# Moving the one-hots ahead of the exps and the column copies in ScalarE's round of a graph attention kernel

## Chip, cores and metric

The kernel runs on one core of one Trainium2 chip. The metric is the device time of one launch in microseconds (us); the time of a kernel is the median of its runs. The kernel before took 1878.13 us (three runs, 1872.55 to 1889.53).

## What is computed

One layer of graph attention with a residual and a layer norm. There are 6250 nodes with 128 features (8 heads of 16) and 206250 edges, sorted by the node they lead to (`dst`). Cut to what matters:

```python
Qh, Kh, Vh = (h @ W for W in (WQ, WK, WV))          # 6250 x 8 x 16 each
Eh = edge_attr @ WE                                  # 206250 x 8 x 16
score = einsum('ehd,ehd,ehd->eh', Kh[src], Qh[dst], Eh) / sqrt(16)
score = exp(clip(score, -5, 5))
msg = Vh[src] * score[:, :, None]
wV, Z = segment_sum(msg, dst), segment_sum(score, dst)
out = layernorm(x + wV / (Z + 1e-6))
```

## The kernel before

**Tiles and rounds.** The edges are cut into 1612 tiles of 128, and these into 406 batches, nearly all of 4 tiles. A table of K and V rows for all nodes (`kv`) is made at the start. Then the loop at L755 makes one round per batch. A round does not finish its batch: the work on a batch is spread over several rounds, so that in round b the engines stand at different batches:

- TensorE (`stage_a`, L608) multiplies the transposed one-hots of batch b with rows of Q into `qps`, and the edge features with WE into `eps`. `stage_0` (L555) makes the marks of batch b-1, one matmul for two batches, so in every second round; `stage_0t` (L588) makes `marks_t` of batch b+2. Marks are numbers that are 1 where an edge leads to a node of the window and not above 0 elsewhere. `finish` (L664) folds the sums of finished windows into one block of 128 nodes (`finps`, mostly 12 or 14 matmul records in the rounds that have it). `stage_c` (L683) adds the messages of batch b-3 into `agg`. `project_columns` (L493) makes K and V of one tile of batch b+2 (`colkv`), and `q_rows` (L341) now and then a block of Q rows (`qrows`).
- VectorE makes `kq` of batch b-1 (L627, L629), sums and clips the scores of batch b-2 (L636, L639) and makes the messages of batch b-3 (`msg`, L678). In between it copies columns of x (L449), splits a block of Q rows (`qst`, L348 to L351) and does pieces of layer norms.
- ScalarE takes the exps of batch b-2 (`weigh`, L642: once into `exp_p`, once beside the messages), copies `colkv` to where batch b+1 expects it (`place_columns`, L503, the copy at L507), copies some 26 columns of x into `xcol` (`columns`, L454), and turns marks into one-hots by a Relu: `mark` (L572, `onehot` of batch b-1 and the next) and `mark_t` (L600, `onehotT` of batch b+2). Behind these come the copy of a fold (`fin`, L671), of a finished pair of windows (`sum`, L711) and of single rows (L491).
- GpSimd gathers rows of `kv` for the tiles of batch b+2 (L518), one indirect DMA per tile. A gather does not start before `qps` of a batch some rounds back is done (L522; the distance shrinks from 12 batches to 3 along the run). SyncE issues the loads.

**Columns.** For 5 of 11 batches the last tile is not gathered. Its 128 source nodes are columns of x that lie on the chip; ScalarE copies 58 of them one by one and VectorE 70 in pairs, and `colkv` is their product with the weights. Columns run ahead: those of a batch are due some four rounds before `project_columns` uses them. Every 16 columns the numbers are read into registers (L420).

**Order and buffers.** From batch 12 on the order of each engine is the order in which the loop's code is written (L758), and each engine works through it strictly. Semaphores set by the framework make an instruction wait for its inputs and for its output's buffer. Four small pools of PSUM matter here: `exp_p` exists once, so the exps of batch b-2 wait for the messages of batch b-3; `eps` once, so it waits for `kq` (L629) of the batch before; `marks_t` once, so it waits for the `onehotT` of the round before. `marks`, `finps`, `colkv` and `qrows` share two buffers in turn (tag `oT`): each waits until what was put there two before has been read, marks by `onehot`, finps by `fin`, colkv by the copy at L507, qrows by `qst` and `qr` on VectorE.

Of the kernel before, what the change touches and what calls it, by code (L numbers as in the profile page):

```python
# [146 lines left out]
def edge_attention(ctx: ExitStack, tc: tile.TileContext, x, xT, srcT, srcA, srcV, srcR, dstT, dstB, dst0, bnd, loB, onB, onQ, eaT,  # L147
# [29 lines left out]
    nbat = len(batches)  # L177
# [9 lines left out]
    with ExitStack() as fast:  # L187
# [167 lines left out]
        def build_q(until, now):  # L355

            while qwork or (now and len(built) < until):
                if not qwork:
                    qwork.append([q_rows(len(built)), 0])
                qwork[0][1] += 1  # L360
                if next(qwork[0][0], None) is None:
                    qwork.pop()
                if not now:
                    break
# [67 lines left out]
        def due(b, v, part):  # L432

            n = int((b + part - 1 - COL0 + COLL) * COLP[1] * share[v] / COLP[0] + 1e-6) // (1 + v) * (1 + v)
            return min(n, len(col_batches) * share[v])

        def copy(v):

            c, (k, i) = copied[v] % COLN, divmod(copied[v], share[v])
            if c == 0:  # L440
                addresses(v)
                at_hand[v] = ahead[v].pop(0)
            copied[v] += 1 + v
            if k not in col_tiles:
                col_tiles[k] = wp.tile([P, P], F32, name="xcol", bufs=6)
            to, at = col_tiles[k], at_hand[v]
            if v:
                i += share[0]
                nc.vector.tensor_tensor(to.bitcast(I32)[:, i:i + 2], column(at[c], 8, I32),  # L449
                                        column(at[c + 1], 8, I32), op=ALU.bitwise_or)  # L450
            else:
                nc.scalar.copy(to[:, i:i + 1], column(at[c], 4, F32))  # L452

        def columns(b, part=1.0):  # L454

            while copied[0] < due(b, 0, part):
                copy(0)
# [45 lines left out]
        def place_columns():  # L503

            while projected:
                g, pk = projected.pop()
                nc.scalar.copy(g[:, B - 1, :], pk)  # L507
# [64 lines left out]
        def mark(b):  # L572

            if b not in marks:
                return
            m, oh, h, n, k = marks.pop(b)
            base = oh[:, h, :n, HW * h:HW * h + HW]
            if k == 2:
                (p_, *dims) = [list(x) for x in base.ap]
                base = bass.AP(tensor=base.tensor, offset=base.offset, ap=[p_, [B * P + HW, 2], *dims])  # L580
                m = m.rearrange("p (k b) w -> p k b w", k=2)
            else:
                m = m[:, :n]
            nc.scalar.activation(base, m, AF.Relu)  # L584
# [3 lines left out]
        def stage_0t(b):  # L588

            if b in marks_t or b in ohTs:  # L590
                return
            t0, n = batches[b][0], len(batches[b])
            m = psM.tile([QROWS, B * P], F32, name="marks_t")
            for i in range(0, n * P, WT * P - t0 % WT * P):
                e0 = (t0 * P + i) % (WT * P)
                w = min(n * P - i, WT * P - e0)
                nc.tensor.matmul(m[:, i:i + w], steps_q, rels[(t0 * P + i) // (WT * P)][:, e0:e0 + w], start=True, stop=True)  # L597
            marks_t[b] = m, n

        def mark_t(b):  # L600

            if b not in marks_t:
                return
            m, n = marks_t.pop(b)
            ohTs[b] = wp.tile([QROWS, B * P], BF16, name="onehotT", bufs=4)
            nc.scalar.activation(ohTs[b][:, :n * P], m[:, :n * P], AF.Relu)  # L606
# [35 lines left out]
        def weigh(b):  # L642

            n, g, sc = st8[b]
            nc.scalar.activation(exp_p[:, :n], sc[:, :n], AF.Exp, scale=0.25)  # L645
            m = wp.tile([P, B, MW], F32, name="msg")
            nc.scalar.activation(m[:, :n, D:], sc[:, :n], AF.Exp, scale=0.25)  # L647
            st8[b] = [n, g, m]
# [15 lines left out]
        def finish(q):  # L664

            ps = psT.tile([P, MW], F32, name="finps", tag="oT")
            add_windows(ps, q, True, True)
            if q % 2 == 0:
                fins[q] = sp.tile([P, 2, MW], F32, name="fin", bufs=2)
            fin = fins[q - q % 2]  # L670
            nc.scalar.copy(fin[:, q % 2], ps)  # L671
            if q % 2:
                q -= 1
                pending.append(layernorm(nc, sp, fins.pop(q), xbs.pop(q), out, q, 2, stores))

        def messages(b):
            n, g, m = st8[b]
            nc.vector.tensor_tensor(  # L678
                m[:, :n, :D].rearrange("p b (h d) -> p b h d", h=H),
                g[:, :n, D:].rearrange("p b (h d) -> p b h d", h=H),  # L680
                exp_p[:, :n, :, None].to_broadcast([P, n, H, DH]), op=ALU.mult)
# [73 lines left out]
        for b in range(nbat + 4):  # L755
# [52 lines left out]
            next(summed, None)  # L808
            if 0 <= b - 3 < nbat:
                messages(b - 3)  # L810
            if 0 <= b - 2 < nbat:
                weigh(b - 2)
            while qwork and b > XB and qwork[0][1] < 3:
                build_q(0, False)
            place_columns()
            if 0 <= b - 1 < nbat:
                stage_0(b - 1)
            if b + 2 < nbat:
                stage_0t(b + 2)
            if b < nbat:  # L820
                columns(b)
            mark(b - 1)
            if b + 2 < nbat:
                mark_t(b + 2)
            for _ in range(len(ready) if b >= nbat - 2 else 1):
                if ready:
                    finish(ready.pop(0))
# [206 lines left out]
```

## Time and profile before

| | |
|---|---|
| median of three runs | 1878.13 us |
| the profiled execution | 1871.11 us, its span 1869.3 us |
| busy, share of the span: PE, VectorE, ScalarE, GpSimd | 80%, 88%, 80%, 73% |
| column copies on ScalarE (L452) | 9802 of 189 ns, 991.4 us |
| onehot (L584), onehotT (L606) on ScalarE | 206 of 577 ns, 406 of 581 ns |
| the exps (L645, L647) | 406 of 199 ns, 406 of 218 ns |
| copy of colkv (L507) | 169 of 358 ns |
| mean granted TensorE clock | 0.931 |

The kernel has three stages: the table (to about 160 us), the rounds with columns (to about 1800 us), and the drain. A row of the waits gives the waiting engine, operation and line, then what ended the wait, and then the total, the number and the longest wait in us. A row of the timeline gives start and length in us, engine, line, operation, what it writes and reads, how many instructions are merged, and in brackets the idle time before it with what ended that. On one engine, neighbours can overlap by about 0.1 us. A row of the windows gives the stretch, its length, busy us (and instructions) of PE, the weight loads PEld, VectorE (DVE), ScalarE (ACT) and GpSimd (POOL), and then the granted clock, the share of DMA time and GB/s.

### The profile page before, as it was taken

To read this page: it belongs to the slowest core of one execution; us is meant where nothing else is said; L and a number is where in the kernel's file an instruction comes from. 1 tells how busy PE (TensorE), PEld (TensorE's weight loads), DVE (VectorE), ACT (ScalarE), POOL (GpSimd) and SP (SyncE) were. 2 spreads that over 40 slices of the span, in tenths; PEclk is the share of its full clock that TensorE was granted. 3 is DMA by queue.
4 is the path that set the end of the run, shared out by engine and by line. 5 is a ranking of instruction groups with operands and counts; after the bars stand their busy time and mean duration, and the time that the engine had idled before them with its cause. 6 is when DMAs were issued, how large, how long until landed. Compare 5 with 4: busy or idle time off the path is not lost.

```text
span 1869.3 us, 54198 instructions
## 1 busy us (share of the span) xinstructions
PE 1499.8 (80%) x10000; PEld 1206.9 (65%) x10000; DVE 1648.0 (88%) x8774; ACT 1495.3 (80%) x11631; POOL 1359.8 (73%) x1433
## 2 busy tenths in 40 slices
PE   6898878878787888888887878877888878777886
PEld 4676657666666666666676666756766656666765
DVE  6468998898889988999989999899899899999986
ACT  3446888788898888898888888888888988988962
POOL 7767767777777776777766777777777777777774
PEclk9888898899899998999989999899989999999897
DMA  8655556556555655655555556556555556566652
GB/s 292 214 163 161 163 173 188 165 179 183 170 178 177 183 172 162 184 180 174 181 173 163 177 174 183 176 167 177 173 174 180 179 175 185 177 178 183 198 153 67
DMA packets 169255, 329.59 MB, mean 176 GB/s; under 512 B 67440, under 2 KB 95156, under 8 KB 168904
## 3 DMA queue, kind: packets, MB, share of 16 engines
q0 software_dynamic: 67664, 183.79, 33.0%
q1 hardware_dynamic: 100115, 141.48, 24.9%
q14 instruction: 272, 2.22, 0.4%
q8 instruction: 80, 1.31, 0.3%
q10 hardware_dynamic: 1124, 0.79, 0.1%
HBM read 309.03 MB, written 16.88 MB: 174 GB/s over the span
## 4 chain that ended last, share of the span: by engine, by line
DVE 34%; ACT 17%; PE 13%; DMA 8%; issue 7%; DVEq 6%; POOL 4%; SPq 2%; ACTq 2%; POOLq 0%
ACT xcol L452 12%; DVE xcol L449 10%; DMA kvrows<-kv,src 7%; DVEq L420 6%; DVE kq L629 5%; DVE sc L636 5%; DVE msg L678 5%; DVE kq L627 5%; POOL kvrows L518 4%; PE agg L700 4%; PE eps L620 3%; ACT onehot L584 2%; PE finps L659 2%; ACT onehotT L606 2%; ACTq L420 1%
## 5 line engine op out<-in xcount | busy, mean ns | idle before, releaser
L518 POOL DMA_INDIRECT kvrows<-kv,src x1378 | 1309.8, 950 | 471.6 <-issue 308.0
L452 ACT COPY xcol<-xz 128x1 f32 x9802 | 991.4, 189 | 76.9 <-issue 66.9
L700 PEld LDWEIGHTS agg<-msg,onehot 128*128 128x128 f32 x3224 | 436.0, 203 | 318.3 <-DVE msg L678 119.1
L449 DVE TENSOR_TENSOR xcol<-xz 128x2 int32 x5915 | 508.9, 152 | 60.5 <-issue 58.3
L620 PE MATMUL eps<-we_sb,ea 128*128 128x128 f32 x3224 | 489.4, 298 | 71.8 <-DVE kq L629 69.8
L700 PE MATMUL agg<-msg,onehot 128*128 128x136 f32 x3224 | 518.5, 307 | 32.3 <-DVE msg L678 30.6
L620 PEld LDWEIGHTS eps<-we_sb,ea 128*128 128x128 f32 x3224 | 424.2, 205 | 100.4 <-DVE kq L629 94.5
L627 DVE TENSOR_TENSOR kq<-kvrows,qps 128x512 f32<-128x512 f32 x406 | 273.8, 674 | 63.5 <-PE qps L615 38.8
L597 PE MATMUL marks_t<-rows_q,steps_q 5*126 5x512 bf16 x406 | 161.8, 399 | 169.5 <-ACT onehotT L606 155.5
L629 DVE TENSOR_TENSOR kq<-kq,eps 128x512 f32<-128x512 f32 x406 | 271.1, 668 | 8.6 <-PE eps L620 6.5
L678 DVE TENSOR_TENSOR msg<-kvrows,exp_p 128x512 f32<-128x512 f32 x406 | 272.7, 672 | 6.2 <-ACT exp_p L645 6.2
L636 DVE TENSOR_REDUCE sc<-kq 128x32 f32<-128x512 f32 x406 | 271.9, 670 | 0.3
L606 ACT ACTIVATE onehotT<-marks_t 126x512 bf16<-126x512 f32 x406 | 235.9, 581 | 19.2 <-PE marks_t L597 18.9
L645 ACT ACTIVATE exp_p<-sc 128x32 f32<-128x32 f32 x406 | 80.9, 199 | 193.9 <-DVE msg L678 191.1
L615 PE MATMUL qps<-qw,onehotT 126*128 126x128 bf16 x1612 | 168.8, 229 | 10.9 <-DVE kq L627 10.9
L615 PEld LDWEIGHTS <-onehotT 126*128 126x128 bf16 x1612 | 134.5, 103 | 47.8 <-issue 21.7
L500 PE MATMUL colkv<-wkv_sb,xcol 128*128 128x256 f32 x338 | 116.2, 429 | 17.2 <-ACT onehot L584 17.2
L584 ACT ACTIVATE onehot<-marks 128x512 f32<-128x512 f32 (+2 forms) x206 | 119.0, 577 | 5.5 <-PE marks L563 5.4
L659 PEld LDWEIGHTS finps<-sum,shift 128*128 128x128 f32 x640 | 81.4, 198 | 40.3 <-ACT kvrows L507 20.9
L659 PE MATMUL finps<-sum,shift 128*128 128x136 f32 x640 | 91.4, 296 | 9.5 <-ACT kvrows L507 9.5
L647 ACT ACTIVATE msg<-sc 128x32 f32<-128x32 f32 x406 | 88.5, 218 | 0.0
L639 DVE TENSOR_SCALAR sc<-sc 128x32 f32<-128x32 f32 x406 | 80.9, 199 | 0.9
(88 smaller groups left out, 799.3 us busy)
## 6 DMA issues: line engine op xcount, KB each, us to landing
ea<-eaT SPq DMA_DIRECT2D x201, 512.0 KB
rowkv<-kv SPq DMA_DIRECT2D x2176, 1.0 KB
kvrows<-kv,src POOLq DMA_INDIRECT x1378
qw<-qs SPq DMA_DIRECT2D x202, 31.5 KB
kv<-ea SPq DMA_DIRECT2D x12, 512.0 KB
qs<-qst SPq DMA_DIRECT2D x48, 96.0 KB
rows_q<-relD SPq DMA_DIRECT2D x202, 6.0 KB
rows<-relO SPq DMA_DIRECT2D x202, 6.0 KB
```

The source lines that it names most:

```text
L449: nc.vector.tensor_tensor(to.bitcast(I32)[:, i:i + 2], column(at[c], 8, I32), column(at[c + 1], 8, I32), op=ALU.bitwise_or)
L452: nc.scalar.copy(to[:, i:i + 1], column(at[c], 4, F32))
L518: ins = nc.gpsimd.indirect_dma_start(out=g[:k, i, :f], out_offset=None, in_=rows, in_offset=bass.IndirectOffsetOnAxis(ap=src_col(t)[:k], a ...
L606: nc.scalar.activation(ohTs[b][:, :n * P], m[:, :n * P], AF.Relu)
L615: expanded[b] = nc.tensor.matmul(pq[:, i, :], ohT[:, i * P:i * P + P], loaded[t0 // WT], start=True, stop=True)
L620: nc.tensor.matmul(pe[:, i, :], ea[:, i * P:i * P + P], we_sb, start=True, stop=True)
L627: nc.vector.tensor_tensor(t0[:, :n], g[:, :n, :D], pq[:, :n], op=ALU.mult)
L629: nc.vector.tensor_tensor(t0[:, :n], t0[:, :n], pe[:, :n], op=ALU.mult)
L636: nc.vector.tensor_reduce(sc[:, :n], t0[:, :n].rearrange("p b (h d) -> p b h d", h=H), axis=AX.X, op=ALU.add)
L659: nc.tensor.matmul(ps, shift[:, P - s:2 * P - s], sums[k // 2][:, k % 2], start=first and i == 0, stop=stop and i == len(parts) - 1)
L678: nc.vector.tensor_tensor(m[:, :n, :D].rearrange("p b (h d) -> p b h d", h=H), g[:, :n, D:].rearrange("p b (h d) -> p b h d", h=H), exp_p[ ...
L700: nc.tensor.matmul(aggs[u][:, 0 if final else k % 2], oh[:, i, :], m[:, i, :], start=not final and t % (2 * G) == 0, stop=tail)
```

## The change

Within a round the calls of `mark` and `mark_t` come ahead of `weigh`, `place_columns` and `columns`. The matmuls that make the marks (`stage_0`, `stage_0t`) keep their place in TensorE's order. `finish` and `stage_c` come behind all of them as before.

```diff
             if 0 <= b - 3 < nbat:
                 messages(b - 3)
-            if 0 <= b - 2 < nbat:
-                weigh(b - 2)
             while qwork and b > XB and qwork[0][1] < 3:
                 build_q(0, False)
-            place_columns()
             if 0 <= b - 1 < nbat:
                 stage_0(b - 1)
             if b + 2 < nbat:
                 stage_0t(b + 2)
-            if b < nbat:
-                columns(b)
             mark(b - 1)
             if b + 2 < nbat:
                 mark_t(b + 2)
+            if 0 <= b - 2 < nbat:
+                weigh(b - 2)
+            place_columns()
+            if b < nbat:
+                columns(b)
             for _ in range(len(ready) if b >= nbat - 2 else 1):
                 if ready:
                     finish(ready.pop(0))
```

The orders of TensorE, VectorE, GpSimd and SyncE are the same in both kernels; only ScalarE's differs. First, ScalarE in the middle of the run, in the round with the marks that are made at 1243 us in the trace and the start of the next round. Before:

```order
L711 COPY sum<-agg 128x272
L645 ACTIVATE exp_p<-sc 128x32
L647 ACTIVATE msg<-sc 128x4x8
L420 TENSOR_LOAD col_at_82
L452 COPY xcol<-xz 128x1 x16
L420 TENSOR_LOAD col_at_82
L452 COPY xcol<-xz 128x1 x11
L584 ACTIVATE onehot_79<-marks 128x2x4x64
L606 ACTIVATE onehotT<-marks_t 126x512
L671 COPY fin<-finps 128x136
L645 ACTIVATE exp_p<-sc 128x32
```

Now:

```order
L711 COPY sum<-agg 128x272
L584 ACTIVATE onehot_79<-marks 128x2x4x64
L606 ACTIVATE onehotT<-marks_t 126x512
L645 ACTIVATE exp_p<-sc 128x32
L647 ACTIVATE msg<-sc 128x4x8
L420 TENSOR_LOAD col_at_82
L452 COPY xcol<-xz 128x1 x16
L420 TENSOR_LOAD col_at_82
L452 COPY xcol<-xz 128x1 x11
L671 COPY fin<-finps 128x136
L606 ACTIVATE onehotT<-marks_t 126x512
```

The same 27 columns now stand behind both one-hots, the copy of the fold follows the columns directly, and the next round begins with its onehotT and not with its exp.

Second, ScalarE in the round whose marks are made at 801 us, where a colkv of the round before is copied. Before:

```order
L452 COPY xcol<-xz 128x1 x4
L606 ACTIVATE onehotT<-marks_t 126x512
L711 COPY sum<-agg 128x272
L645 ACTIVATE exp_p<-sc 128x32
L647 ACTIVATE msg<-sc 128x4x8
L507 COPY kvrows<-colkv 128x256
L452 COPY xcol<-xz 128x1 x12
```

Now:

```order
L452 COPY xcol<-xz 128x1 x4
L711 COPY sum<-agg 128x272
L584 ACTIVATE onehot_77<-marks 128x2x4x64
L606 ACTIVATE onehotT<-marks_t 126x512
L645 ACTIVATE exp_p<-sc 128x32
L647 ACTIVATE msg<-sc 128x4x8
L507 COPY kvrows<-colkv 128x256
L452 COPY xcol<-xz 128x1 x12
```

Between the columns of one round and the copy of colkv (L507) in the next stood one onehotT, of the round before; now onehot and onehotT of the round itself stand there.

## Prediction

> **What bounds the kernel now.** I read the page first, then the busy times of the long middle stage in one piece (160 to 1800 us: all but the table at the start and the drain), then the waits inside that stage, and last the timeline of single rounds.
>
> ```profile
> span 1869.3 us, 54198 instructions
> 160.00:1800.00 1640.00, 1325.01 (x9004) 1068.49 (x9005) 1502.95 (x8411) 1413.58 (x11398) 1205.76 (x1271) 0.94 0.59 176
> DVE xcol L449 <- issue: 56.6, 112, 1.3
> DVE qst L348 <- PE qrows L344: 36.7, 28, 2.5
> DVE kq L627 <- PE qps L615: 25.5, 25, 2.6
> ACT exp_p L645 <- DVE msg L678: 146.8, 123, 4.1
> PE marks_t L597 <- ACT onehotT L606: 154.3, 161, 2.3
> PE qrows L344 <- ACT onehot L584: 21.0, 17, 2.3
> PE colkv L500 <- ACT onehot L584: 17.2, 17, 2.2
> 1001.75 0.95 POOL L518 DMA_INDIRECT kvrows<-kv,src  x1 [0.30 <-issue]
> 1003.00 0.94 POOL L518 DMA_INDIRECT kvrows<-kv,src  x1 [0.30 <-issue]
> ```
>
> In the second row the columns after the length are PE, PEld, DVE, ACT and POOL busy. VectorE works 1503 of 1640 us and spends 57 more on reading column numbers into registers ("issue"). What is left of its idle time is almost only two waits: qst for qrows and kq for qps, 36.7 + 25.5 = 62.2 us. It hardly ever waits for ScalarE directly. GpSimd stands close behind: a gather starts every 1.25 us (1001.75 to 1003.00), and 1271 of them fill 1589 us, so the stage cannot become more than about 51 us shorter however well the rest runs. ScalarE waits 147 us for VectorE and has room. So the time is VectorE's work plus the 62 us in which it waits for TensorE, and the question is what the new order on ScalarE does to those 62 us. TensorE's 154 us of waiting for onehotT is the largest number here, but TensorE is busy 1325 of 1640 us and most of that wait is covered: only what reaches qst or kq counts.
>
> **The change part by part.** Nothing is added or removed; every instruction of TensorE, VectorE, GpSimd and SyncE keeps its place. On ScalarE the ring of work is almost the same ring; what differs is that the one-hots of this round now stand ahead of the exps, so they are a round's columns earlier, and exps, the copy of colkv (L507) and columns stand behind them. A fold (finps) and its copy (fin) keep their place behind the columns.
>
> I sorted rounds 31 to 379 by what TensorE issues in them and added up the two VectorE waits that follow each kind. Where the waits are large, TensorE has a long round, because finps, colkv or qrows come on top. The first kind, ten rounds with finps and colkv, 13.1 us in all, looks like this:
>
> ```profile
> 1243.11 0.38 PE L563 MATMUL marks<-steps,rows 26*128 26x512 bf16 x1
> 1243.13 0.68 DVE L678 TENSOR_TENSOR msg<-kvrows,exp_p 128x512 f32<-128x512 f32 x1
> 1243.64 1.66 PE L659 MATMUL finps<-sum,shift 128*128 128x136 f32 x12
> 1245.14 1.09 PE L700 MATMUL agg<-msg,onehot 128*128 128x136 f32 x8
> 1247.11 0.67 DVE L678 TENSOR_TENSOR msg<-kvrows,exp_p 128x512 f32<-128x512 f32 x1
> 1247.75 0.58 ACT L584 ACTIVATE onehot<-marks 128x512 f32<-128x512 f32 x1
> 1248.24 0.57 ACT L606 ACTIVATE onehotT<-marks_t 126x512 bf16<-126x512 f32 x1
> 1248.39 0.70 PE L500 MATMUL colkv<-wkv_sb,xcol 128*128 128x256 f32 x2 [2.16 <-ACT onehot L584]
> 1249.35 0.69 DVE L627 TENSOR_TENSOR kq<-kvrows,qps 128x512 f32<-128x512 f32 x1 [1.57 <-PE qps L615]
> ```
>
> The marks are ready at 1243.49, but their one-hot comes at 1247.75 behind 27 columns, and colkv needs its PSUM buffer. With the one-hot first it starts near 1243.5, colkv at 1246.2 behind agg, and kq at 1247.8 instead of 1249.35. Over the ten rounds I leave 4.6 us (two are late for other reasons): **-8.5 us**.
>
> ```profile
> 244.45 0.29 DVE L348 CAST qst<-qrows 128x128 bf16<-128x128 f32 x1 [0.93 <-PE qrows L344]
> 1706.86 0.29 DVE L348 CAST qst<-qrows 106x128 bf16<-106x128 f32 x1 [0.47 <-PE qrows L344]
> 365.17 0.29 DVE L348 CAST qst<-qrows 128x128 bf16<-128x128 f32 x1 [2.09 <-PE qrows L344]
> 1598.59 0.29 DVE L348 CAST qst<-qrows 128x128 bf16<-128x128 f32 x1 [2.00 <-PE qrows L344]
> 1018.26 0.51 PE L344 MATMUL qrows<-wq_sb,xz 128*128 128x128 f32 x2
> 1017.95 0.26 ACT L671 COPY fin<-finps 128x136 f32<-128x136 f32 x1
> ```
>
> The first two rows are the first and last of twelve rounds with colkv and qrows and no finps, 11.2 us: here qrows takes the buffer of the marks, the same cure holds: agg and colkv behind one msg and then qrows take some 2.4 us, and the next msg, behind which qst stands, ends 4 us later (1243.81 and 1247.78 above), so nothing is left: **-11 us**. The next two are the first and last of eight rounds that have finps, colkv and qrows, 15.8 us. There qrows takes the buffer of finps, and the last two rows show it start as soon as fin ends (1018.21). fin stays behind the columns. Counted from the end of the last columns, three one-hots stood ahead of it (onehotT, then the exps and columns, then onehot and onehotT) and now two do; each takes 0.49 (1247.75 to 1248.24). So fin comes 0.5 us earlier, eight times: **-4 us** of 15.8.
>
> A third sort of wait has nothing to do with long rounds:
>
> ```profile
> 316.00:318.00 2.00, 0.28 (x3) 0.22 (x2) 2.00 (x15) 1.81 (x15) 1.70 (x2) 1.00 0.72 234
> 320.00:322.00 2.00, 2.00 (x11) 1.64 (x10) 0.75 (x3) 1.96 (x16) 1.47 (x2) 0.50 0.44 126
> 318.44 0.37 PE L597 MATMUL marks_t<-rows_q,steps_q 5*126 5x512 bf16 x1 [2.16 <-ACT onehotT L606]
> 321.92 0.69 DVE L627 TENSOR_TENSOR kq<-kvrows,qps 128x512 f32<-128x512 f32 x1 [1.25 <-PE qps L615]
> ```
>
> TensorE waits 2.16 us for onehotT, its granted clock (third number from the end in the windows) then falls to 0.50, the products take nearly twice as long, and kq is late. Fourteen rounds of this sort hold 11.2 us. The wait at marks_t goes, since onehotT of the round before is now done before that round's columns. Bounds: nothing, if the slow clock alone makes kq late, and 11.2; I take half, **-5.5 us**, as in this row the wait is larger than what kq loses.
>
> Now the price. In 23 rounds finps takes the buffer of the last colkv and waits for ScalarE's copy L507 (upper rows: one of fifteen plain cases):
>
> ```profile
> 801.05 0.39 PE L563 MATMUL marks<-steps,rows 26*128 26x512 bf16 x1
> 801.78 0.20 ACT L645 ACTIVATE exp_p<-sc 128x32 f32<-128x32 f32 x1 [0.76 <-DVE msg L678]
> 801.92 0.21 ACT L647 ACTIVATE msg<-sc 128x32 f32<-128x32 f32 x1
> 802.04 0.35 ACT L507 COPY kvrows<-colkv 128x256 f32<-128x256 f32 x1
> 802.44 1.89 PE L659 MATMUL finps<-sum,shift 128*128 128x136 f32 x14 [0.79 <-ACT kvrows L507]
> 804.76 0.68 DVE L678 TENSOR_TENSOR msg<-kvrows,exp_p 128x512 f32<-128x512 f32 x1
> 805.58 0.69 DVE L627 TENSOR_TENSOR kq<-kvrows,qps 128x512 f32<-128x512 f32 x1
> ```
>
> ```profile
> 1748.94 0.37 ACT L507 COPY kvrows<-colkv 128x256 f32<-128x256 f32 x1
> 1750.02 0.38 PE L563 MATMUL marks<-steps,rows 26*128 26x512 bf16 x1
> ```
>
> Before, the exp starts when msg ends, at 801.78. Now onehot can start only at 801.44, when the marks are made, onehotT follows 0.49 later and the exp another 0.49 behind it, at 802.42: L507 ends 0.64 later than it did, and finps, agg, qps and kq shift with it, because kq already starts right behind msg here (805.44) with TensorE just in time. 23 x 0.64 = 14.7 us. In eight of the 23, TensorE was behind and L507 was over about when the marks began or before (the last of the eight is the lower pair); those lose up to 1.5 us, and I add 0.5 each: **+19 us**. The bounds are nothing (TensorE, freed of its waits, is early enough) and 23 x 1.5 = 35 us.
>
> The exps are later by the same 0.64 in rounds with marks. That is hidden: msg at 804.76 needs the second exp of 802.13, 2.6 us earlier. Without that cover it would cost 0.64 in every second round, over 100 us; I take **+2 us** for rounds in which ScalarE is already late. What else is queued behind the waiting onehot is the columns, ready some four rounds ahead of their use, and fin.
>
> The clock is the last term. The stage's mean granted clock is 0.94, so TensorE runs some 197 us at half speed (1640 x 0.06 x 2). Fewer waits should mean fewer such spells; between nothing and the 5.7 us left over above, I take **-4 us**. [...]
>
> Sum: -8.5 - 11 - 4 - 5.5 + 19 + 2 - 4 = -12 us. The profiled execution took 1871.1 us, 1.8 of it outside the span; so 1859 for such an execution. The median of the three runs shown is 1878.1, 7 us above it, and 12 off that median is **1866 us**, 0.6% less.
>
> **The rivals.** *The folds lose nothing* (0.22): TensorE, without the 154 us of waits and with the other 38 us for onehot gone, starts a fold's round early enough, and the +19 and +2 stay away; with half of the eight rounds behind fin cured as well (-4 more) and the clock better, 35 to 40 us go. For it: those waits are in four rounds of ten. Against it: the marks themselves come right behind eps, whose start VectorE sets, so in a round like that at 801 us TensorE cannot be earlier. 1840 us.
>
> *The clock decides* (0.12): if half of the 197 us at half speed disappear, the fourteen slow rounds lose all their 11.2 us and the long rounds gain another few; -12 becomes -20 to -24, 1856 us. [...] Against it: TensorE's work is the same, so its share of idle time hardly changes; waits for VectorE take the place.
>
> *ScalarE is now tied to TensorE* (0.16), the case on the other side: every exp, copy and column stands behind one-hots that wait for eps and marks. If the marks come 1 us or more behind msg (TensorE late, clock at 0.50) in the 23 folds, each loses the full 1.5 us (+35); in the ten rounds with finps and colkv and the eight behind fin the later fold eats the 12.5 us gained, and the slow rounds and the clock give nothing. Only -11 remain of the gains, and +24 us give 1902. With these gains gone it passes no change from 0.5 us per fold (11 / 23) and 1% from 1.3. For it: the order is exactly this. Against it: the row at 801 us, a plain one, gives 0.64.
>
> *It does nothing that shows*: the terms cancel. This lies inside my forecast, whose sum is small against its parts.
>
> **How the numbers follow.** My forecast has 0.50; its own range, with the fold term between 8 and 27 and the slow rounds between 0 and 11 us, is 1852 to 1880. The range takes in the first rival and half of the other side: 1839 to 1889. A measurement of this kernel can tell about 1% (19 us, below 1859 or above 1897). Faster by more: the first rival's 0.22, two thirds of the clock's 0.12 and 0.08 from the lower edge of the forecast, 0.38. Slower by more: the third rival without its lower edge, 0.14. Same: 0.48.
>
> **What would show it.** Right: PE marks_t waits for onehotT almost vanish (154 to under 20 us); colkv and qrows hardly wait for onehot; qst for qrows falls from 36.7 to about 20; finps waits longer than 0.79 us for L507 in a round like that at 801 us; ScalarE's wait before the exp shrinks and a new one appears before onehot and onehotT, for marks and marks_t; kq for qps stays near 20. Wrong: VectorE's msg waits for exp_p by more than 15 us, or gathers wait for nothing but issue (GpSimd the bound), or the qst wait stays.

## The result, and the profile after

| | before | changed |
|---|---|---|
| median of six runs each | 1880.20 us (1867.80 to 1889.53) | 1850.13 us (1842.04 to 1857.83) |
| ratio, 95% interval | | 0.986 [0.983, 0.989] |
| the profiled execution, its span | 1871.11, 1869.3 us | 1855.70, 1853.7 us |
| its mean granted TensorE clock | 0.931 | 0.911 |

The changed kernel is 1.4% faster. The forecast said 1866 us, 0.6% faster than the runs shown; the time lies inside its widest range (1839 to 1889) and beyond the 1% that can be told from no change. The outcome that the forecast thought likeliest, no change that can be told (0.48), did not come; "faster" had 0.38. The two profiled executions understate the difference: the one before lies 9 us below its median, the one after 6 us above.

First the page's span and the middle stage of the changed kernel in one piece (columns as in the prediction: busy PE, PEld, DVE, ACT, POOL, then the clock, DMA share, GB/s):

```profile
span 1853.7 us, 54385 instructions
160.00:1800.00 1640.00, 1370.17 (x9085) 1108.45 (x9083) 1511.59 (x8436) 1411.14 (x11395) 1217.00 (x1283) 0.92 0.59 178
```

In the same 1640 us VectorE is now busy 1511.6 us where it was 1503.0, and 12 more gathers are through (1283 for 1271). TensorE's busy time went up by 45 us, for little more work: its clock fell from 0.94 to 0.92.

The waits of that stage in the changed kernel (waiting engine, operation and line, what ended it; total, number, longest):

```profile
ACT onehotT L606 <- PE marks_t L597: 115.1, 81, 3.6
ACT onehot L584 <- PE marks L563: 62.8, 63, 3.1
DVE xcol L449 <- issue: 55.9, 99, 2.4
DVE qst L348 <- PE qrows L344: 25.4, 18, 2.7
PE finps L659 <- ACT onehot L584: 19.9, 23, 1.8
DVE kq L627 <- PE qps L615: 16.7, 12, 2.7
PE qrows L344 <- ACT fin L671: 14.0, 8, 2.1
DVE kq L627 <- DMA kvrows<-kv,src: 8.7, 9, 2.3
ACT exp_p L645 <- DVE msg L678: 4.7, 16, 0.9
```

VectorE's two waits, qst and kq for TensorE, fell from 62.2 to 42.1 us. The rows of colkv and qrows waiting for onehot (17.2 and 21.0 us before) are gone. ScalarE's wait has moved, as it had to: 146.8 us in front of the exp became 4.7, and 178 us stand in front of the one-hots. And there is a row that was not there: **finps waits for onehot, in 23 rounds**. Before, those 23 folds took colkv's buffer, and 15 of them waited for the copy L507 (9.5 us in all).

Two groups of the changed kernel's page, over the whole run (busy, mean ns, then the idle time just before and what ended it):

```profile
L597 PE MATMUL marks_t<-rows_q,steps_q 5*126 5x512 bf16 x406 | 170.9, 421 | 0.2
L678 DVE TENSOR_TENSOR msg<-kvrows,exp_p 128x512 f32<-128x512 f32 x406 | 273.1, 673 | 6.5 <-ACT exp_p L645 6.4
```

marks_t waits 0.2 us where it waited 154 for onehotT, and the later exps show nowhere: VectorE's messages wait 6.4 us for them in the whole run.

How the waits make up the time can be read from rounds 31 to 379. They are sorted by what TensorE issues on top in them, as in the prediction; each cell is the sum of VectorE's waits before qst and kq in the rounds of that kind, whatever ended them, added up from the rows of the timeline. Kinds that hold next to nothing are left out, so the last sum is a little above its column. "Changed, again" is a second profile of the changed kernel; "onehotT alone" (the second run of that kernel) and "copy first" belong to experiments below.

| kind of round (number) | before | changed | changed, again | onehotT alone | the same, copy first |
|---|---|---|---|---|---|
| finps and colkv (10) | 13.1 | 7.5 | 10.1 | 19.6 | 20.8 |
| colkv and qrows (12) | 11.2 | 0.8 | 0.0 | 20.4 | 19.6 |
| finps, colkv and qrows (8) | 15.8 | 14.4 | 13.8 | 16.6 | 17.6 |
| finps, or finps and qrows, behind a colkv (23 folds) | 13.8 | 19.4 | 12.9 | 49.2 | 29.1 |
| colkv without either (128) | 11.2 | 6.9 | 5.7 | 3.1 | 2.7 |
| all rounds | 65.2 | 52.6 | 47.1 | 112.0 | 92.7 |
| length of rounds 31 to 379 | 1539.7 | 1521.3 | 1516.9 | 1578.4 | 1550.4 |
| clock of that execution | 0.931 | 0.911 | 0.923 | 0.912 | 0.919 |

Of the 18.4 and 22.8 us by which the stretch became shorter, 12.6 and 18.1 are these waits; the rest is VectorE's idle time elsewhere, mostly for reading column numbers (some 3 and 2 us less), and some 2 us of work.

**A round that was cured.** One of the ten rounds with finps and colkv, like the one at 1243 us before; timeline of the changed kernel:

```profile
1302.21 0.39 PE L563 MATMUL marks<-steps,rows 26*128 26x512 bf16 x1
1302.63 0.60 ACT L584 ACTIVATE onehot<-marks 128x512 f32<-128x512 f32 x1 [0.64 <-PE marks L563]
1302.74 1.66 PE L659 MATMUL finps<-sum,shift 128*128 128x136 f32 x12
1304.23 1.09 PE L700 MATMUL agg<-msg,onehot 128*128 128x136 f32 x8
1305.16 0.59 PE L500 MATMUL colkv<-wkv_sb,xcol 128*128 128x256 f32 x2
1306.55 0.67 DVE L627 TENSOR_TENSOR kq<-kvrows,qps 128x512 f32<-128x512 f32 x1
```

onehot stands right behind the marks, colkv starts behind agg without a wait, and kq follows 4.34 us after the marks; it was 6.24 (1243.11 to 1249.35).

**And one of the same kind that was not.** Its timeline, and a window over it:

```profile
1197.61 0.60 PE L563 MATMUL marks<-steps,rows 26*128 26x512 bf16 x1
1198.57 3.23 PE L659 MATMUL finps<-sum,shift 128*128 128x136 f32 x14
1201.64 1.09 PE L700 MATMUL agg<-msg,onehot 128*128 128x136 f32 x8
1203.42 0.69 DVE L627 TENSOR_TENSOR kq<-kvrows,qps 128x512 f32<-128x512 f32 x1 [2.19 <-PE qps L615]
```

```profile
1198.00:1201.40 3.40, 3.40 (x14) 2.84 (x13) 3.21 (x21) 3.15 (x24) 2.49 (x4) 0.51 0.54 127
```

Nothing waits for onehot here either. TensorE runs at a clock of 0.51, its finps takes 3.23 us for 14 matmuls, where the 14 of the next fence take 1.89, and kq is 2.19 us late. Five of the ten rounds are of this sort, with a mean clock of 0.50 to 0.55 and 2.9 us and more from finps to agg; four of them hold all of the 7.5 us that this kind still loses. In the kernel before two of the ten ran like that, in the second profile of the changed kernel six.

**A fold.** The round that answers to the one at 801 us before:

```profile
803.34 0.39 PE L563 MATMUL marks<-steps,rows 26*128 26x512 bf16 x1
803.76 0.60 ACT L584 ACTIVATE onehot<-marks 128x512 f32<-128x512 f32 x1 [1.18 <-PE marks L563]
804.25 0.59 ACT L606 ACTIVATE onehotT<-marks_t 126x512 bf16<-126x512 f32 x1
804.41 1.89 PE L659 MATMUL finps<-sum,shift 128*128 128x136 f32 x14 [0.47 <-ACT onehot L584]
804.97 0.37 ACT L507 COPY kvrows<-colkv 128x256 f32<-128x256 f32 x1
806.14 1.09 PE L700 MATMUL agg<-msg,onehot 128*128 128x136 f32 x8
807.04 0.67 DVE L678 TENSOR_TENSOR msg<-kvrows,exp_p 128x512 f32<-128x512 f32 x1
807.64 0.67 DVE L627 TENSOR_TENSOR kq<-kvrows,qps 128x512 f32<-128x512 f32 x1
```

L507 ends 2.00 us after the marks began (805.34), 0.66 later than before: the forecast's 0.64. But finps does not wait for it. It starts at the end of onehot, 1.07 us after the marks, where it started 1.39 after them before, and kq has no wait. finps can start before L507 has read colkv, so it stands in the other buffer, that of the marks. In every order run here finps waits for whichever of `mark` and `place_columns` is written first: for onehot in the four profiles with `mark` first, for L507 in all others. From this it is inferred, not read from the framework, that a new tile takes the buffer that is given back first in the order of the code. What was said ahead of the prediction, that a tile waits for what was put into the buffers two before, therefore holds for finps in the kernel before and not in the changed one.

### The profile page after: what moved, and what is told of

Same layout as the page of the kernel before. It is cut to its first block, busy times and chain, and to the rows that moved or that the text cites. A ratio compares the mean times of both kernels' runs of the same rounds, so it can differ in the third digit from the quotient of the medians.

```text
span 1853.7 us, 54385 instructions
## 1 busy us (share of the span) xinstructions
PE 1533.8 (83%) x10000; PEld 1239.4 (67%) x10000; DVE 1646.3 (89%) x8774; ACT 1488.8 (80%) x11631; POOL 1360.4 (73%) x1433
## 4 chain that ended last, share of the span: by engine, by line
DVE 40%; ACT 14%; PE 14%; DVEq 6%; DMA 5%; issue 4%; POOL 2%; ACTq 1%; SPq 0%; POOLq 0%
DVE xcol L449 12%; ACT xcol L452 9%; DVE kq L629 7%; DVEq L420 6%; DVE sc L636 6%; DVE kq L627 6%; DVE msg L678 5%; DMA kvrows<-kv,src 5%; PE eps L620 4%; PE agg L700 3%; PE finps L659 3%; POOL kvrows L518 2%; ACT onehotT L606 2%; DVE sc L639 1%; ACT onehot L584 1%
## 5 line engine op out<-in xcount | busy, mean ns | idle before, releaser
L700 PEld LDWEIGHTS agg<-msg,onehot 128*128 128x128 f32 x3224 | 442.5, 206 | 240.6 <-issue 129.7
L620 PE MATMUL eps<-we_sb,ea 128*128 128x128 f32 x3224 | 504.8, 304 | 110.1 <-DVE kq L629 104.8
L620 PEld LDWEIGHTS eps<-we_sb,ea 128*128 128x128 f32 x3224 | 433.3, 209 | 150.4 <-DVE kq L629 139.9
L606 ACT ACTIVATE onehotT<-marks_t 126x512 bf16<-126x512 f32 x406 | 238.3, 587 | 147.3 <-PE marks_t L597 146.8
L629 DVE TENSOR_TENSOR kq<-kq,eps 128x512 f32<-128x512 f32 x406 | 271.4, 669 | 8.9 <-PE eps L620 6.9
L597 PE MATMUL marks_t<-rows_q,steps_q 5*126 5x512 bf16 x406 | 170.9, 421 | 0.2
L659 PE MATMUL finps<-sum,shift 128*128 128x136 f32 x640 | 109.1, 332 | 20.3 <-ACT onehot L584 19.9
L659 PEld LDWEIGHTS finps<-sum,shift 128*128 128x128 f32 x640 | 97.2, 230 | 42.7 <-ACT onehot L584 30.4
L500 PE MATMUL colkv<-wkv_sb,xcol 128*128 128x256 f32 x338 | 109.8, 409 | 0.0
```

Source lines behind the costliest of these rows:

```text
L620: nc.tensor.matmul(pe[:, i, :], ea[:, i * P:i * P + P], we_sb, start=True, stop=True)
L629: nc.vector.tensor_tensor(t0[:, :n], t0[:, :n], pe[:, :n], op=ALU.mult)
L659: nc.tensor.matmul(ps, shift[:, P - s:2 * P - s], sums[k // 2][:, k % 2], start=first and i == 0, stop=stop and i == len(parts) - 1)
L700: nc.tensor.matmul(aggs[u][:, 0 if final else k % 2], oh[:, i, :], m[:, i, :], start=not final and t % (2 * G) == 0, stop=tail)
```

## The experiments

The reference for each is a run of the kernel before on the same chip. Letters: P is `place_columns` (L507), M `mark`, T `mark_t`, W `weigh`, C `columns`, H half of the columns, F the loop of `finish`. The kernel before runs W P C M T F, the changed one M T W P C F. Two theories of the gain stood against each other: that onehot, early, frees the shared buffers (the rounds with colkv), or that onehotT, early, takes TensorE's 154 us of waits away, and with them slow clock. And the fold term, the largest of the forecast, had to be found or shown absent.

| order on ScalarE | median, us | ratio to before, 95% |
|---|---|---|
| M W P C T F (onehot alone) | 1858.75 | 0.987 [0.982, 0.992] |
| T W P C M F (onehotT alone) | 1910.44 | 1.018 [1.015, 1.021] |
| T W P C M F, a second time | 1905.84 | 1.018 [1.014, 1.021] |
| P T W C M F | 1886.04 | 1.006 [1.004, 1.009] |
| M T W P C F (changed), a second time | 1850.11 | 0.985 [0.981, 0.990] |
| P M T W C F | 1846.27 | 0.981 [0.978, 0.985] |
| P M T W H F C | 1839.07 | 0.980 [0.976, 0.983] |
| P M W H T F C | 1835.56 | 0.979 [0.975, 0.983] |
| P W H M T F C | 1833.38 | 0.978 [0.974, 0.982] |
| changed, marks_t computed twice | 1867.24 | 0.996 [0.993, 0.998] |

### The changed kernel once more

The edit is none: it stood beside the later runs, as the reference for them.

> The changed kernel unaltered, for a second profile beside the others of this set. If the profiled pair overstated nothing but the granted clock (0.931 before, 0.911 after): ratio 0.983 to 0.989 again, a mean clock within 0.006 of the kernel before, and in runs of one kernel 6 to 10 us less for each 0.01 of clock.

It took 1850.11 us, 0.985 [0.981, 0.990]; its profiled execution 1851.73 us at a clock of 0.923. Its column of the table of rounds shows what repeats and what does not: the kind with colkv and qrows is free of waits both times, while the folds lie 5.6 us above the kernel before in one execution and 0.9 below it in the other.

### onehot alone

```diff
             mark(b - 1)
-            if b + 2 < nbat:
-                mark_t(b + 2)
             if 0 <= b - 2 < nbat:
                 weigh(b - 2)
             place_columns()
             if b < nbat:
                 columns(b)
+            if b + 2 < nbat:
+                mark_t(b + 2)
```

(Against the changed kernel, as all diffs here unless said otherwise.)

> Only onehot (of batch b-1) stands ahead of the exps; onehotT stays behind the columns as before. If the gain comes from the PSUM buffer that marks hold (colkv and qrows wait for onehot): those waits, 38 us before, fall under 8, the twelve rounds with colkv and qrows lose their 11 us, and the time is 0.986 to 0.992 of before, most of the changed kernel's 0.986. TensorE's wait of marks_t for onehotT stays near 150 us and costs little. If the gain comes from that wait instead: ratio 0.996 to 1.002. If the granted clock decides: the ratio follows the clock, whichever waits go.

Waits of its middle stage:

```profile
PE marks_t L597 <- ACT onehotT L606: 148.9, 174, 3.9
DVE qst L348 <- PE qrows L344: 23.1, 18, 3.3
DVE kq L627 <- PE qps L615: 22.6, 18, 2.7
PE finps L659 <- ACT onehot L584: 10.3, 23, 0.7
```

TensorE still waits 148.9 us for onehotT, as before (154.3), and yet the kernel is 1.3% faster; its interval (0.982 to 0.992) and that of the changed kernel (0.983 to 0.989, and 0.981 to 0.990 the second time) overlap nearly whole. So the largest wait of the profile of before was worth nothing that shows at this spread, and the gain is that of onehot: no row of qrows or colkv waiting for onehot is left, and the twelve rounds with colkv and qrows hold no wait of VectorE at all. The 23 folds wait for onehot here too: it is `mark` ahead of `place_columns` that does it.

### onehotT alone

```diff
-            mark(b - 1)
             if b + 2 < nbat:
                 mark_t(b + 2)
...
             if b < nbat:
                 columns(b)
+            mark(b - 1)
```

> Only onehotT stands ahead of the exps; onehot stays behind the columns. If the buffer of marks is the cause: marks_t's wait of 154 us falls under 20 and still the time is 0.993 to 1.001 of before, since qrows and colkv go on waiting for onehot (30 to 40 us) and only the rounds at a low clock gain. If the wait for onehotT is the cause: 0.986 to 0.990.

```profile
ACT onehotT L606 <- PE marks_t L597: 218.5, 134, 4.0
DVE qst L348 <- PE qrows L344: 59.5, 30, 3.6
PE finps L659 <- ACT kvrows L507: 37.3, 23, 2.8
PE qrows L344 <- ACT onehot L584: 31.2, 14, 4.0
```

The wait of marks_t is gone here, and the kernel is 1.8% slower. The folds are the forecast's: with `mark` behind `place_columns` again, finps waits 23 times for L507, which is later than before. One such fold, from the second run of this kernel:

```profile
819.62 0.39 PE L563 MATMUL marks<-steps,rows 26*128 26x512 bf16 x1
821.00 0.36 ACT L507 COPY kvrows<-colkv 128x256 f32<-128x256 f32 x1
821.41 1.89 PE L659 MATMUL finps<-sum,shift 128*128 128x136 f32 x14 [1.18 <-ACT kvrows L507]
823.13 1.09 PE L700 MATMUL agg<-msg,onehot 128*128 128x136 f32 x8
```

finps starts 1.79 us after the marks and agg 3.51 after them; in the changed kernel it was 1.07 and 2.80, in the kernel before 1.39.

### onehotT alone, with the copy first

That kernel with L507 put ahead of everything tells whether the loss is the gate at the folds or onehotT itself in front of the exps. Diff against onehotT alone:

```diff
+            place_columns()
             if b + 2 < nbat:
                 mark_t(b + 2)
             if 0 <= b - 2 < nbat:
                 weigh(b - 2)
-            place_columns()
```

> ScalarE's round is copy of colkv, onehotT, exps, columns, onehot: the kernel with onehotT alone moved (1.0175 of the time before), with the copy L507 put ahead of everything else. Two explanations of that loss differ here. (1) The folds: in that kernel finps waited 37.3 us for L507, 23 times, and VectorE's waits for TensorE in the 23 fold rounds were 54.2 us, 40 above the kernel before. With L507 first, finps must wait for it less than 12 us, the fold rounds must fall back to 10 to 20 us of VectorE's waits, and the ratio to 0.995 to 1.003; qst for qrows stays above 30 us, since onehot stands last. (2) ScalarE tied to TensorE by onehotT itself, which stands ahead of the exps and waits for marks_t: the copy's place changes little, onehotT waits for marks_t over 150 us as before, and the ratio stays at 1.01 or above.

This run says little: on its chip the kernel before took 2556 us, and this one 2585 (1.012 [1.007, 1.017]). It was taken again, on another chip, beside onehotT alone:

> The same kernel as the run before it (copy of colkv, onehotT, exps, columns, onehot), unaltered: that run fell on a chip on which the kernel before itself took 2556 us at a granted clock of 0.766, so that its waits cannot be read against the others. The two explanations stand as they were. (1) The folds: finps waits less than 12 us for L507, VectorE's waits in the 23 fold rounds are 10 to 20 us, the ratio 0.995 to 1.003. (2) ScalarE tied to TensorE by onehotT itself: onehotT waits over 150 us for marks_t, the ratio stays at 1.01 or above.

> The kernel with onehotT alone moved (onehotT, exps, copy of colkv, columns, onehot), unaltered, on the same chip as the one with the copy first, so that the two are compared directly. By both explanations it takes 1.014 to 1.021 of the time before, with some 37 us of finps waiting for L507; by the folds the kernel with the copy first is 1.5 to 2% faster than this one, by ScalarE tied to TensorE within 0.7% of it.

The kernel with the copy first took 1886.04 us and the one without 1905.84, against 1877.18 before. Waits of the kernel with the copy first:

```profile
ACT onehotT L606 <- PE marks_t L597: 169.2, 128, 3.5
DVE qst L348 <- PE qrows L344: 53.5, 30, 3.2
PE qrows L344 <- ACT onehot L584: 40.8, 20, 4.3
PE finps L659 <- ACT kvrows L507: 16.4, 13, 2.1
```

Neither expectation was met in full. The copy's place gives back 20 of the 29 us that onehotT alone had lost; the waits at the folds fall by the same 20, from 49.2 to 29.1 us. The gate at the folds is thus some two thirds of that loss. The 9 us that remain are not the folds alone: qst still waits 53.5 us (36.7 before), because onehot stands last and qrows and colkv wait for it, and the rounds with colkv beside finps or qrows hold 18 us more than before (58.0 for 40.1). Waits grew by 27 us in all and the stretch by only 11, since VectorE's idle time elsewhere, mostly for reading column numbers, was some 11 us less and its busy time 5 us less.

### The copy first, in the changed order

```diff
+            place_columns()
             mark(b - 1)
             if b + 2 < nbat:
                 mark_t(b + 2)
             if 0 <= b - 2 < nbat:
                 weigh(b - 2)
-            place_columns()
```

> The changed kernel with the copy of colkv (L507) ahead of the one-hots, so that a fold finds a buffer that ScalarE gives back before it turns to the marks. If folds behind ScalarE's one-hots still cost time in the changed kernel: finps's wait for ScalarE (20 us on TensorE, 23 times) falls under 5 and the time is 2 to 8 us below the changed kernel, 0.981 to 0.985 of before. If TensorE's clock or VectorE's own work sets those rounds: no difference from the changed kernel, 0.986.

1846.27 us, 0.981 [0.978, 0.985]; its interval and that of the changed kernel overlap. finps waits for L507 again, 9.1 us where under 5 was expected, but less than the 19.9 us for onehot in the changed kernel, since the copy now comes early:

```profile
PE finps L659 <- ACT kvrows L507: 9.1, 12, 1.7
```

So the order decides both which buffer a fold gets and when that is free; either buffer will do if it is given back early. VectorE's waits in the 23 fold rounds are 8.7 us here, against 19.4 and 12.9 in the changed kernel. That the time is lower is not shown: kq's wait for qps is 34.4 us (16.7 and 19.4 there), and the ten rounds with finps and colkv hold 16.0, six of them near half clock.

### The fold in the middle of the columns

What was left in the changed kernel was qrows waiting for fin behind a round's columns (14.0 us). Here, and in the next two, fin comes after half of them:

```diff
+            place_columns()
             mark(b - 1)
...
-            place_columns()
             if b < nbat:
-                columns(b)
+                columns(b, 0.5)
             for _ in range(len(ready) if b >= nbat - 2 else 1):
                 if ready:
                     finish(ready.pop(0))
+            if b < nbat:
+                columns(b)
```

> As the one before, and the fold's copy fin stands in the middle of the columns instead of behind them. If the eight rounds in which qrows takes the buffer of finps still wait for fin: qst's wait for qrows falls from 25 to 10 to 15 us, qrows's wait for fin from 14 us to under 3, and the time is another 6 to 12 us less, 0.975 to 0.981 of before. If the wait only moves (fin then waits for finps on TensorE, or qrows is late behind agg anyway): 0.983 to 0.987.

```profile
DVE qst L348 <- PE qrows L344: 7.9, 10, 2.0
PE qrows L344 <- ACT fin L671: 3.2, 6, 0.8
```

1839.07 us, 0.980 [0.976, 0.983]. The wait of qrows for fin falls from 14.0 to 3.2 us and that of qst from 25.4 to 7.9 (13.5 and 16.6 with the copy first alone), while kq still waits 29.6 us for qps. The waits thus fall as expected; that the fold's place alone makes the run shorter is not clear of noise (0.976 to 0.983, against 0.978 to 0.985 with the copy first).

### The one-hots in the middle too

```diff
-            mark(b - 1)
-            if b + 2 < nbat:
-                mark_t(b + 2)
+            place_columns()
             if 0 <= b - 2 < nbat:
                 weigh(b - 2)
-            place_columns()
             if b < nbat:
-                columns(b)
+                columns(b, 0.5)
+            mark(b - 1)
+            if b + 2 < nbat:
+                mark_t(b + 2)
             for _ in range(len(ready) if b >= nbat - 2 else 1):
                 if ready:
                     finish(ready.pop(0))
+            if b < nbat:
+                columns(b)
```

> Copy of colkv, exps, half of the columns, onehot, onehotT, fold, rest of the columns. If what counts is that one-hots and fold give their PSUM buffers back before the end of the columns, and one-hots at the head only tie ScalarE to TensorE: ScalarE waits for marks and marks_t under 30 us (178 in the changed kernel), marks_t for onehotT under 40, qst and kq for TensorE under 40 together, time 0.974 to 0.982 of before, at or below the best so far (0.980). If the one-hots must be first: 0.984 to 0.990.

Waits from 160 to 1790 us, as this run is shorter:

```profile
ACT exp_p L645 <- DVE msg L678: 137.5, 131, 3.6
DVE kq L627 <- PE qps L615: 19.0, 15, 3.9
DVE kq L627 <- DMA kvrows<-kv,src: 15.6, 12, 2.2
DVE qst L348 <- PE qrows L344: 6.9, 11, 2.2
```

1833.38 us, 0.978 [0.974, 0.982], the lowest median of all; the slowest of its six runs (1838.80) is faster than the fastest of the changed kernel on that chip (1840.42). ScalarE again waits at the exp (137.5 us) and not at the one-hots, as in the kernel before. So the gain does not need the one-hots first; it is enough that onehot, and then fin, come before a full round of columns. VectorE's waits in rounds 31 to 379 fall to 34.9 us. kq now waits 15.6 us for gathers: the bound named in the prediction begins to show.

With only onehotT in the middle and onehot ahead of the exps:

```diff
+            place_columns()
             mark(b - 1)
-            if b + 2 < nbat:
-                mark_t(b + 2)
             if 0 <= b - 2 < nbat:
                 weigh(b - 2)
-            place_columns()
             if b < nbat:
-                columns(b)
+                columns(b, 0.5)
+            if b + 2 < nbat:
+                mark_t(b + 2)
             for _ in range(len(ready) if b >= nbat - 2 else 1):
                 if ready:
                     finish(ready.pop(0))
+            if b < nbat:
+                columns(b)
```

> Copy of colkv, onehot, exps, half of the columns, onehotT, fold, rest of the columns. By the same theory 0.974 to 0.982, ScalarE still waiting some 60 us for marks; if onehotT behind onehot at the head is free, as the changed kernel suggests, no better than copy first with the fold in the middle, 0.978 to 0.983.

1835.56 us, 0.979 [0.975, 0.983]: the same. With the fold in the middle, onehotT's place makes no difference that shows among these three, nor does onehot's, as long as no whole round of columns comes before it.

### More work for TensorE

The matmul of marks_t is issued twice, to the same place; nothing is left out.

```diff
-                nc.tensor.matmul(m[:, i:i + w], steps_q, rels[(t0 * P + i) // (WT * P)][:, e0:e0 + w], start=True, stop=True)
+                for _ in range(2):
+                    nc.tensor.matmul(m[:, i:i + w], steps_q, rels[(t0 * P + i) // (WT * P)][:, e0:e0 + w], start=True, stop=True)
```

> The changed kernel with the matmul of marks_t issued twice into the same place, 406 more matmuls of about 0.4 us on TensorE. If TensorE's clock falls because it idles: the mean granted clock rises by 0.02 or more over the changed kernel's, and the time is within 8 us of it or below. If its load lowers the clock, or the clock does not depend on so small a change: clock the same or lower, and the time 12 to 25 us longer, since the extra 0.4 us counts in some forty long rounds and behind ScalarE's wait for marks_t.

1867.24 us, 17 us above the changed kernel on the same chip. Its mean clock over all runs is 0.917, the changed kernel's there 0.921. TensorE was busy for 1430.7 of the 1640 us from 160 to 1800, where it was 1352.3 in the second profile of the changed kernel, and the clock did not rise.

## Why the prediction was right or wrong

Terms of the sum against the two profiles of the changed kernel, from the table of rounds:

| term | forecast | measured, first and second profile |
|---|---|---|
| rounds with finps and colkv | -8.5 | -5.6, -3.0 |
| rounds with colkv and qrows | -11 | -10.4, -11.2 |
| rounds with finps, colkv and qrows | -4 | -1.4, -2.0 |
| slow rounds | -5.5 | -4.3, -5.5 |
| **folds** | **+19** | **+5.6, -0.9** |
| exps later | +2 | msg's wait 6.4 us, 6.2 before |
| clock | -4 | 0.911 and 0.923, 0.931 before |

**The step that failed** is the price: "In 23 rounds finps takes the buffer of the last colkv and waits for ScalarE's copy L507", which "ends 0.64 later than it did, and finps, agg, qps and kq shift with it". The delay of L507 was right (0.66 in the round shown). That finps still hangs on it was read from the kernel before and not asked again for the new order. In the changed kernel all 23 folds wait for onehot. In the plain case they start 0.32 us earlier against the marks; over all 23 they start 1.47 and 1.36 us after them (first and second profile), where it was 1.18. The fifteen that had waited for L507 went from 1.48 to 1.38 and 1.25; the eight for which L507 had been over went from 0.62 to 1.63 and 1.55, nearly what the forecast gave these eight, but behind onehot. Where the gate at L507 did stay, in onehotT alone, the folds cost 35 us more than before (49.2 against 13.8), the upper bound that the forecast gave. What the folds still lose in the first profile goes with two things in the timeline: eight of the 23 have a mean clock of 0.50 to 0.72 from finps to agg (one before, four in the second profile), and in twelve onehot starts 0.76 to 1.80 us after the marks and not 0.42, because ScalarE is still at the round before. The term is a sum of opposite signs: the 14 folds without qrows hold 9.6 and 6.6 us where they held 3.3, the nine with qrows 9.8 and 6.3 where they held 10.6.

**The rounds with colkv and qrows** went as forecast, and so did their reason. **Those with finps and colkv** lost their wait for onehot: colkv waits for nothing in any of the ten. But some lose time at half clock instead. In the other kernels with onehot ahead of a full round of columns this kind holds 8.7 to 16.8 us (13.1 before), so its gain is not shown beyond that scatter. **Those with qrows behind fin** gained some 0.2 us each (1.4 and 2.0 over eight) where 0.5 was forecast. In such a round fin still comes behind the columns, and only the fold in their middle cured it (3.0 to 5.0 us in the three kernels that have it).

**The slow rounds** gained the half that was taken, but perhaps only in part by the cause that stood there: with onehot alone, where marks_t still waits 148.9 us, the rounds with colkv and nothing else on top hold 9.1 us, between the 11.2 of before and the 6.9 and 5.7 of the changed kernel. That the wait of marks_t is worth 2 to 3 us in them is argued from single profiles, not shown.

**The clock** was forecast to get better, and did not. No run shows the -4 of that term; that fewer waits mean fewer spells at half clock was the author's estimate. Half-clock spells in the records of the two profiles came to 259 us in 47 spells before and 334 us in 55 after (287 in 48 in the second). The waits for onehotT that went away were replaced by waits for VectorE (agg for msg from 29.3 to 98.2 us, eps for kq from 64.2 to 100.5), as the forecast had said against its own second rival, "the clock decides".

**The sum.** With the measured fold term in place of +19, the forecast's -12 becomes -25 to -32. The profiles moved by 15.4 and 19.4 us, since the gains of the rounds with finps and of the clock came in part or not at all. The medians moved by 30.1 and 25.2 (1875.32 before on the second chip). Between the two lies the clock: the profiled execution of before had the highest of the three, and a kernel's time goes with it, by some 7 us per 0.01 (last section). Median to median, the forecast of -12 was 13 to 18 us short. That the time lies in the stated range is in part luck: the forecast's own range was given as 1852 to 1880 (by its own terms, 8 for the folds and -11 for the slow rounds, its lower end is 1849.5), and the first rival, which widened it to 1839, had another reason than the one that came.

**The rivals.** "The folds lose nothing" had the right outcome for the folds, and its 1840 us is 10 us below the measured time where the forecast is 16 above it; but its reason, a TensorE that comes early enough, is not what happened. "ScalarE is now tied to TensorE" did not come for this change. It came in the kernel with onehotT alone: 1910 us, with its price of 1.5 us per fold (35.4 over 23), and 20.1 of the 35.4 gave way when the copy moved. That nothing shows is excluded by the interval.

**What was to show it.** marks_t's wait for onehotT went (0.2 us), colkv and qrows no longer wait for onehot, qst fell to 25.4 and 19.6 us, the exp's wait moved to the one-hots, kq stayed near 20: right. finps waiting longer than 0.79 us for L507 in a round like that at 801 us: wrong, it waits 0.47 us, for onehot. None of the signs named as wrong appeared.

## What to carry to other kernels

When tiles of several kinds share a few buffers in turn, reordering one engine can change which tile gets which buffer: work out the pairing again in the new order before a wait of the old trace is priced. The largest wait of an engine that is not the bound (154 us here) can go or stay without a trace in the time, while an operation of 0.58 us behind a long row of small copies, which empties a buffer that another engine needs, was worth 1.3%. And such an operation need not be first in its round: the version with the lowest median put it after half the row.

## What the runs showed of the hardware

**The granted clock wanders from run to run of one kernel, and about half of the spread of its time goes with it.** In 41 runs of the kernel before, on three chips, the mean clock lay between 0.909 and 0.933 and the time between 1865 and 1886 us; a straight line through them gives 7.4 us per 0.01 of clock (correlation -0.74). Twelve runs of the changed kernel give 7.3 (-0.75). Which of the two drives the other, such a line does not say. Mean clocks are 0.925 before and 0.920 after; at equal clock, by that line, the change is worth an estimated 31 us (1877.1 + 7.4 x 0.49 = 1880.7, less 1849.6).

**TensorE was not idle ahead of its half-clock spells.** In the records of the two profiles all but one spell in each (46 of 47 before, 54 of 55 after) are 3.41 us long or a multiple of it, up to 17.07 us. The 3.41 us ahead of the spell that the prediction shows in its row from 320 us (it begins at 319.11), from the kernel before:

```profile
315.70:319.11 3.41, 1.25 (x10) 0.89 (x9) 3.41 (x21) 3.22 (x27) 2.67 (x3) 1.00 0.63 209
```

TensorE is busy for 1.25 of 3.41 us. Ahead of the 41 spells that begin in the middle stage of that trace it was busy for 20 to 66% of the 3.41 us, in 20 of them for 50% or more; ahead of the 50 of the changed kernel for 17 to 67%. A low share alone does not decide it: of the stage's stretches of 3.41 us at full clock, counted on from the start of a spell, in which it was busy for less than 66%, 40 were followed by half clock and 59 by full clock in the kernel before, 48 and 23 in the changed one. What else decides was not shown. The prediction's reading, that fewer waits give a better clock, did not hold here at this size: neither 154 us of waits less nor 406 matmuls more raised it.

**On one chip the kernels took a third longer, while the instructions of VectorE, ScalarE and GpSimd kept their length.** There the kernel before took 2556 us at a clock of 0.766 in its runs. The page of the kernel with onehotT and the copy first, on that chip:

```profile
L518 POOL DMA_INDIRECT kvrows<-kv,src x1378 | 1308.3, 949 | 1182.6 <-issue 348.9
L627 DVE TENSOR_TENSOR kq<-kvrows,qps 128x512 f32<-128x512 f32 x406 | 275.6, 679 | 241.4 <-PE qps L615 132.6
```

A gather takes 949 ns and kq 679, as the same kernel on the other chip (951 and 674); ScalarE's column copies take 189 ns on both. A matmul of eps takes 345 ns where it took 302, at the lower clock. The idle time in front of gather and kq is 1182.6 and 241.4 us, where it was 480.5 and 72.5. Two kinds of wait stand out in its trace: ScalarE's column copies stood idle for 356.5 us behind nothing that the profile shows (36.5 on the other chip), and 587 us of waits of all engines were ended by something that it cannot name (on its page 177.1 of them before kq at L629), where the other chip has none. The cause stays open.
